# Layer 0 of a four-layer graph network: the order of key and value projections, bias halves and loads in its opening

## The chip, the cores and the metric

The kernel runs on one core of a Trainium2 chip. The metric is the device time of one execution in microseconds (us). The core has five engines that run side by side, each in its own order: PE (TensorE) multiplies matrices, DVE (VectorE) and ACT (ScalarE) do elementwise work and empty PE's accumulators, POOL (GpSimd) does some elementwise work and issues DMAs, SP (SyncE) only issues DMAs. Matrix products land in PSUM, a small accumulator memory; everything else on the chip lies in SBUF.

## What is computed

Four layers are applied in turn to a node matrix x of 4096 x 256 with a dense stored adjacency matrix adj of 4096 x 4096 (under 1% of its entries are not zero). Each layer's result is added to its input and normalized by row. Only the first layer is touched by the change:

```python
qkv = x @ Wqkv + bqkv                         # q, k, v: 4096 x 256 each, 4 heads of 64
scores = einsum('hnd,hmd->hnm', qh, kh) * 64 ** -0.5
scores = scores + graph_bias * adj
scores = where(adj == 0, -1e9, scores)
out = einsum('hnm,hmd->hnd', softmax(scores), vh)
x = layernorm(x + out @ Wout + bout)
```

(In the source the mask and the adjacency are two arguments; both are adj.) The second layer is a graph attention with one score per node and neighbour, the third and fourth multiply by the adjacency with normalized rows and columns.

## The kernel before, in words

**Tiles of layer 0.** The nodes are cut into 32 chunks of 128 query rows (class `Rows`, one per chunk). Two heads make a pair, so a chunk has two pairs (class `Pair`), and there are 64 units of work. The 4096 key columns are cut into four stretches of 1024, `k` = 0 to 3. One step is one unit and one stretch: 256 steps, and a few more to let the pipeline run out.

**What a step does.** `step(t)` writes out the order of the work by hand; the whole runs under `tc.manual_schedule()`, so each engine executes its instructions in the order in which the program issues them, and waits where one is not ready. Step t computes the scores of its own unit and stretch (`score`, L366: eight matmul records into two PSUM tiles), which DVE adds to the bias, writes to SBUF and takes the maximum of (L375, two instructions for two heads). Four steps behind, ACT takes exponentials (`expo`, L391); five steps behind, PE transposes them and ACT copies them out of PSUM (`turn`, L405 and L413); six steps behind, PE multiplies them by the values (`attend`, L423). So the first exponentials come in step 4, the first transposes in step 5, and the first attention in step 6.

**Bias rows.** Scores need, for each chunk, the bias `graph_bias * adj` with the mask. `Rows.load(k)` (L256) loads one stretch of the adjacency's rows in four DMAs on SP of 128 KB each, into one of two `raw` buffers. `make_bias(k, half)` handles half a stretch: DVE transposes it (L272), finds the zeros (L277) and forms the bias (L278). `make_edges` then lets ACT make a copy in bf16 for layer 1 and a row sum (L289) into one of two `mk` buffers, and POOL writes that to memory (L295). Bias tiles come from a pool of seven buffers, one of which holds the key and value weights `wkv_sb` as long as they are needed. From step 0 on, each step also makes half a stretch of the next chunk's bias.

**Queries.** `Rows.fetch` (L302, L306) loads the chunk's columns of the transposed x, `xq`, and its rows `xr`. `Rows.begin` projects the queries (L313, eight matmul records) into PSUM buffer `po1`, DVE moves them out with bias and scale (L321), and POOL adds the output bias to `xr` (L329).

**Keys and values.** They are projected from x in eight pieces of 512 nodes. `load_x(mb)` (L199) loads a piece of 512 KB on SP into one of five buffers. `project(mb)` computes two halves of the keys (L210, eight matmul records, PSUM buffers `po0` and `po1`), which ACT copies with the bias into `store` (L217; the first half serves pair 0), and then the values (L226, sixteen records, PSUM buffer `tr`), which DVE moves out with their bias (L233). The transposed exponentials use the buffer `tr` too.

**The opening before step 0.** SP gets, in this order: piece 0 of x, the weights `wkv_sb`, the first raw set of chunk 0, piece 1, the second raw set, `xq` and `xr`, pieces 2 and 3. Small constants, the query weights and the output weights go through ACT's queue. Then come the queries of chunk 0, and all eight bias halves of chunk 0, with `project(0)` and `project(1)` behind the second and the fourth half. In steps 1 to 3, ahead of the scores:

```python
if t > 0:
    for mb in range(2 * t, min(2 * t + 2, N // 512)):
        project(mb)
```

So step t's scores find all keys of their stretch, and pieces 2 to 7 stand in steps 1 to 3. `project(mb)` ends with the load of piece mb + 4.

Of the kernel before, what the change touches and what calls it, by code (L numbers as in the profile page):

```python
# [17 lines left out]
N = 4096  # L18
# [8 lines left out]
NS = N // TS  # L27
# [17 lines left out]
def tile_gnn(  # L45
# [123 lines left out]
    with ExitStack() as l0:  # L169
# [25 lines left out]
        x_in = {}  # L195

        def load_x(mb):
            xt = pp_.tile([P, 2, 512], F32, tag="pt", name="xt")
            nc.sync.dma_start(  # L199
                xt, xT[:, mb * 512 : (mb + 1) * 512].rearrange("(c p) m -> p c m", p=P)  # L200
            )
            x_in[mb] = xt

        def project(mb):

            xt = x_in.pop(mb)
            for pr in range(2):
                pk = ps_o.tile([P, 512], F32, tag=f"po{pr}", name="pk")
                for cc in range(2):
                    nc.tensor.matmul(  # L210
                        pk,
                        wkv_sb[:, cc, pr * P : (pr + 1) * P],
                        xt[:, cc, :],
                        start=(cc == 0),
                        stop=(cc == 1),
                    )
                nc.scalar.activation(  # L217
                    kT[:, pr, mb * 512 : (mb + 1) * 512],
                    pk,
                    AF.Identity,  # L220
                    bias=bqk_sb[:, 2 + pr : 3 + pr],
                )
            pv = ps_t.tile([P, 4, D], F32, tag="tr", name="pv")
            for s in range(4):
                for cc in range(2):
                    nc.tensor.matmul(  # L226
                        pv[:, s, :],
                        xt[:, cc, s * P : (s + 1) * P],
                        wkv_sb[:, cc, D : 2 * D],
                        start=(cc == 0),  # L230
                        stop=(cc == 1),
                    )
            nc.vector.tensor_tensor(  # L233
                v_sb[:, mb * 4 : (mb + 1) * 4, :],
                pv,
                bv_b.unsqueeze(1).to_broadcast([P, 4, D]),
                ALU.add,
            )
            if mb + 4 < N // 512:
                load_x(mb + 4)  # L240

        class Rows:

# [212 lines left out]
        rows = [Rows(ib) for ib in range(NCH)]  # L456
# [5 lines left out]
        def step(t):  # L462
            unit, k = divmod(t, NS)
            ib, pr = divmod(unit, 2)
            live = t < n_steps
            ua, ka = divmod(t - LA, NS)
            tag_a, tag_o = f"po{ua % 2}", f"po{1 - ua % 2}"
            ut, kt = divmod(t - LT, NS)
            ue, ke = divmod(t - LE, NS)
            attends = 0 <= ua < n_units  # L470
            turns = 0 <= ut < n_units
            expos = 0 <= ue < n_units
            grow = live and ib + 1 < NCH
            if grow and pr == 0 and k == NS - 1:
                rows[ib + 1].fetch()
            if ua > 0 and ka == 0:
                pairs[ua - 1].scale()
            if t > 0:
                for mb in range(2 * t, min(2 * t + 2, N // 512)):
                    project(mb)  # L480
            if live:
                if k == 0:
                    pairs[unit] = Pair(rows[ib], pr)
                pairs[unit].score(k)
            if expos:
                pairs[ue].expo(ke, 0)
            if turns:
                pairs[ut].turn(kt, 0)
            if expos:
                pairs[ue].expo(ke, 1)  # L490
            if attends:
                pairs[ua].attend(ka, tag_a)
                if ka == NS - 2:
                    pairs[ua].sums()
                if ka == NS - 1:
                    pairs[ua].norm(tag_o)
            if ua > 0 and ka == 1:
                if ua % 2 == 0:
                    pairs[ua - 1].rows.finish(tag_o)
                del pairs[ua - 1]  # L500
            if grow:
                if pr == 1 and k == NS - 2:
                    rows[ib + 1].begin(tag_o if attends else "po1")
                kb, half = divmod(pr * NS + k, 2)
                if edges:
                    edges.pop().make_edges()
                edges.append(rows[ib + 1])
                rows[ib + 1].make_bias(kb, half)
                if half == 0 and kb + 1 < NS:
                    rows[ib + 1].load(kb + 1)  # L510
                elif half == 0 and ib + 2 < NCH:
                    rows[ib + 2].load(0)
            elif edges:
                edges.pop().make_edges()
            if turns:
                pairs[ut].turn(kt, 1, by_dve=not live)
            for f, *args in tail.get(t, ()):
                f(*args)
# [98 lines left out]
        def first_es():  # L617
# [30 lines left out]
                (first_es,),  # L648
            ],
        }  # L650
        with tc.manual_schedule():
            load_x(0)
            nc.sync.dma_start(wkv_sb, wqkv[:, D:].rearrange("(c p) e -> p c e", p=P))
            rows[0].load(0)
            load_x(1)
            rows[0].load(1)
            rows[0].fetch()
            load_x(2)
            load_x(3)
            nc.scalar.dma_start(wout_sb, wout.rearrange("(c p) e -> p c e", p=P))  # L660
            nc.scalar.dma_start(bout_b, bout.partition_broadcast(P))
            rows[0].begin("po1")
            for k in range(NS):
                for half in range(2):
                    rows[0].make_bias(k, half)
                    rows[0].make_edges()
                if k < 2:
                    project(k)
                if k + 2 < NS:
                    rows[0].load(k + 2)  # L670
                elif k + 2 == NS:
                    rows[1].load(0)
            for t in range(n_steps + LA + 2):
                step(t)

# [444 lines left out]
```

## Time and profile before

| What | Value |
| --- | --- |
| Runs | 2788.17 us median of 3 (2787.74 to 2789.93) |
| Profiled execution | 2790.52 us, of which the span from first to last instruction is 2788.7 us |
| Busy share of the span | PE 98%, DVE 80%, ACT 59%, POOL 8% |
| First PE instruction | at 20.20 us |
| Start of the scores of steps 0, 1, 2, 3 | 36.69, 54.76, 70.65, 86.54 us |
| Start of the scores of step 7 | 107.38 us |

Times in the profile count from the first instruction. "x8" is a count of instructions, "L210" a line of the kernel, and `pk<-xt,wkv_sb` names what is written and read. Each matrix product in float32 appears as two matmul records. Matmuls overlap in PE's pipeline and their ends are modelled, so the busy time of a group can reach past the start of the next. The time in brackets is how long the engine was idle before the group, with what ended that idleness. The granted clock is the share of TensorE's full clock.

### The profile page before, as it was taken

What the parts mean: (1) busy time and instruction counts of PE and PEld (TensorE: products, weight loads), DVE (VectorE), ACT (ScalarE), POOL (GpSimd) and SP (SyncE); (2) the same over time, 40 slices, a digit from 0 to 9 for tenths busy, and PEclk for the clock granted to TensorE, in tenths of its full rate; (3) what the DMA queues carried; (4) which work ended last, traced back from release to release, by engine and by line L of the source; (5) the groups of instructions that cost most, each with busy time, mean ns of one, the idle gap of its engine ahead of it and who ended that gap; (6) DMA issues with size and microseconds to landing.
All of it is one profiled execution on the core that took longest, in us unless ns stands there. A gap on an engine that the chain in (4) does not pass through costs nothing.

```text
span 2788.7 us, 57962 instructions
## 1 busy us (share of the span) xinstructions
PE 2720.9 (98%) x23568; PEld 1862.4 (67%) x23568; DVE 2225.5 (80%) x4059; ACT 1655.4 (59%) x2675; POOL 234.3 (8%) x404
## 2 busy tenths in 40 slices
PE   6999999999999999999997999999999999999997
PEld 4677777777777777777786888886444444444443
DVE  4799999999988999999858888885866577676565
ACT  2699999999999999999857777772100001000000
POOL 1111111111111111111100000000200000000000
PEclk9999999999999999999999999999999999999998
DMA  6344444444444444444362222212555555555552
GB/s 156 63 83 86 93 87 85 89 90 83 87 92 83 88 89 84 90 87 87 95 202 70 77 77 76 76 43 90 176 158 170 162 159 157 164 168 175 181 169 73
DMA packets 671291, 308.01 MB, mean 110 GB/s; under 512 B 547376, under 2 KB 577456, under 8 KB 671024
## 3 DMA queue, kind: packets, MB, share of 16 engines
q1 hardware_dynamic: 655776, 265.10, 38.7%
q0 software_dynamic: 13440, 37.77, 3.5%
q8 instruction: 184, 3.01, 0.5%
q10 hardware_dynamic: 1808, 1.44, 0.2%
q14 instruction: 83, 0.68, 0.1%
HBM read 258.21 MB, written 46.01 MB: 109 GB/s over the span
## 4 chain that ended last, share of the span: by engine, by line
PE 93%; issue 3%; DVE 1%; DMA 1%; ACT 1%; SPq 0%; POOL 0%; DVEq 0%; POOLq 0%; ACTq 0%
PE m L948 27%; PE po L423 17%; PE po L770 16%; PE sc L366 16%; PE ptr L405 10%; PE py L982 2%; PE pq L313 1%; PE pp L335 1%; PE pb L441 1%; PE pk L210 1%; PE pv L226 1%; DMA mk<-edge 1%; SPq L256 0%; DMA x<-xs 0%; DVE z L375 0%
## 5 line engine op out<-in xcount | busy, mean ns | idle before, releaser
L375 DVE CUSTOM_DVE_ANT_0 z<-sc,bias 128x1024 f32<-128x1024 f32 x512 | 605.9, 1221 | 40.5 <-PE sc L366 39.0
L391 ACT ACTIVATE z<-z,nm 128x1024 f32<-128x1024 f32 x512 | 590.2, 1153 | 6.7 <-DVE nm L387 6.7
L413 ACT COPY pt<-ptr 128x1024 f32<-128x1024 f32 x507 | 511.4, 1009 | 99.3 <-PE ptr L405 89.9
L366 PE MATMUL sc<-store,qT 64*128 64x512 f32 x2048 | 506.7, 608 | 1.6 <-DVE mx L375 1.5
L423 PE MATMUL po<-pt,xc 128*64 128x128 f32 x8192 | 504.2, 276 | 0.0
L770 PE MATMUL po<-store,pt 128*128 128x257 f32 x2048 | 447.2, 380 | 12.6 <-issue 12.6
L423 PEld LDWEIGHTS po<-pt,xc 128*64 128x64 f32 x8192 | 442.3, 137 | 17.6 <-DVE pt L411 0.2
L405 PEld LDWEIGHTS ptr<-ident,z 64*128 64x128 f32 x8192 | 322.3, 138 | 177.8 <-issue 78.4
L770 PEld LDWEIGHTS po<-store,pt 128*128 128x128 f32 x2048 | 388.6, 190 | 70.9 <-issue 12.7
L948 PE MATMUL m<-asum,ysum 128*128 128x512 f32 x768 | 356.6, 594 | 6.3 <-issue 6.3
L405 PE MATMUL ptr<-ident,z 64*128 64x64 f32 x8192 | 356.3, 225 | 5.8 <-ACT pt L413 4.4
L366 PEld LDWEIGHTS sc<-store,qT 64*128 64x128 f32 x2048 | 192.9, 189 | 119.4 <-issue 109.2
L948 PEld LDWEIGHTS m<-asum,ysum 128*128 128x128 f32 x768 | 146.0, 190 | 177.9 <-issue 160.9
L948 PE MATMUL m<-asum,store 128*128 128x512 f32 x512 | 263.2, 596 | 0.0
L948 PE MATMUL m<-a,ysum 128*128 128x512 f32 x512 | 245.9, 594 | 0.0
L295 POOL DMA_DIRECT2D edge<-mk x256 | 145.4, 568 | 1004.5 <-ACT mk L289 981.1
L954 ACT COPY e<-m 128x512 f32<-128x512 f32 x32 | 18.5, 586 | 351.6 <-PE m L948 351.6
L917 DVE TENSOR_TENSOR asum<-a 128x512 f32<-128x512 f32 x128 | 88.1, 688 | 163.9 <-PE m L948 163.9
L724 ACT ACTIVATE z<-z,es_q 128x1024 f32<-128x1024 f32 x128 | 146.5, 1145 | 120.5 <-DVE mx L711 111.9
L278 DVE SCALAR_TENSOR_TENSOR bias<-rt,gb,u 128x512 f32<-128x512 f32 x256 | 194.2, 759 | 9.1
L760 DVE STREAM_TRANSPOSE pt<-z 128x1024 f32<-128x1024 f32 x128 | 158.1, 1237 | 41.7 <-PE po L770 41.7
L948 PEld LDWEIGHTS m<-asum,store 128*128 128x128 f32 x512 | 97.8, 191 | 123.3 <-issue 121.4
(123 smaller groups left out, 2561.5 us busy)
## 6 DMA issues: line engine op xcount, KB each, us to landing
a<-in_adjT SPq DMA_DIRECT2D x256, 512.0 KB, 5.1
raw<-in_adjT SPq DMA_DIRECT2D x512, 128.0 KB, 4.0
edge<-mk POOLq DMA_DIRECT2D x256, 128.0 KB, 2.5
mk<-edge SPq DMA_DIRECT2D x256, 128.0 KB, 2.9
xt<-in_xT SPq DMA_DIRECT2D x8, 512.0 KB, 5.4
xq<-in_xT SPq DMA_DIRECT2D x32, 128.0 KB, 3.9
xr<-in_x SPq DMA_DIRECT2D x32, 128.0 KB, 3.1
x<-xs POOLq DMA_DIRECT2D x8, 512.0 KB, 4.1
```

The source lines that it names most:

```text
L278: nc.vector.scalar_tensor_tensor(self.bias[k][:, m0 : m0 + HT], rt, gb, u, ALU.mult, ALU.add)
L295: nc.gpsimd.dma_start(edge[self.ib * P : (self.ib + 1) * P, k * TS + m0 : k * TS + m0 + HT], mk)
L366: nc.tensor.matmul(ps[j][:, q * 512 : (q + 1) * 512], self.rows.qT[j * HD : (j + 1) * HD, self.pr, :], kT[j * HD : (j + 1) * HD, self.pr, ...
L375: nc.vector.tensor_tensor_reduce(z, ps[j], self.rows.bias[k], 1.0, NEG, ALU.add, ALU.max, self.mx[:, j, k : k + 1],)
L391: nc.scalar.activation(z, z, AF.Exp, bias=self.nm[:, j : j + 1], accum_out=self.ls[:, j, k : k + 1],)
L405: nc.tensor.transpose(pa[:, r, c, :], z[half, c * P : (c + 1) * P], ident[half, half])
L413: nc.scalar.copy(to, pa)
L423: nc.tensor.matmul(self.po[j * HD : (j + 1) * HD, 0:P], v_sb[:, ci, h * HD : (h + 1) * HD], self.pt[j][k][:, c, :], start=(ci == 0), stop= ...
L724: nc.scalar.activation(self.z[s], self.z[s], AF.Prelu, bias=self.eq[:, s : s + 1], alpha=SLOPE)
L760: nc.vector.transpose(self.pt[:, :, s, :], self.z[s].rearrange("p (b r) -> p b r", r=QB))
L770: nc.tensor.matmul(self.po[:, 0 : D + 1], self.pt[:, b, :, :].rearrange("p s i -> p (s i)"), wh[:, b, :], start=(b == 0), stop=(b == NBK - 1),
L948: nc.tensor.matmul(self.m[i], left, right, start=(c == 0), stop=(c == NP - 1))
```

## The change

`project` is split into `project_k` (keys) and `project_v` (values). Before step 0, SP's queue gets `xq` and `xr` before piece 1, and five pieces of x instead of four; `project_v(mb)` then loads piece mb + 5. Before step 0 the kernel projects the keys of pieces 0 and 1, with the queries of chunk 0 between them, and makes two bias halves instead of eight. The other six, all values and the keys of pieces 2 to 7 are put into a plan for steps 0 to 4, which `step` executes directly behind the step's scores. The first raw set of chunk 1 is asked for before step 0 as before, but ahead of the third and fourth of chunk 0, which follow in steps 0 and 1; chunk 1's second set follows at the end of step 1 and its third at the end of step 2.

```diff
-        def project(mb):
-
-            xt = x_in.pop(mb)
+        def project_k(mb):
+
+            xt = x_in[mb]
             for pr in range(2):
                 pk = ps_o.tile([P, 512], F32, tag=f"po{pr}", name="pk")
...
                     AF.Identity,
                     bias=bqk_sb[:, 2 + pr : 3 + pr],
                 )
+
+        def project_v(mb):
+
+            xt = x_in.pop(mb)
             pv = ps_t.tile([P, 4, D], F32, tag="tr", name="pv")
...
-            if mb + 4 < N // 512:
-                load_x(mb + 4)
+            if mb + 5 < N // 512:
+                load_x(mb + 5)
...
-            if t > 0:
-                for mb in range(2 * t, min(2 * t + 2, N // 512)):
-                    project(mb)
             if live:
                 if k == 0:
                     pairs[unit] = Pair(rows[ib], pr)
                 pairs[unit].score(k)
+            for f, *args in plan.get(t, ()):
+                f(*args)
             if expos:
                 pairs[ue].expo(ke, 0)
...
                 rows[ib + 1].make_bias(kb, half)
-                if half == 0 and kb + 1 < NS:
+                if t < NS:
+
+                    if t == 1:
+                        rows[0].load(3)
+                    if 0 < t < 3:
+                        rows[1].load(t)
+                elif half == 0 and kb + 1 < NS:
                     rows[ib + 1].load(kb + 1)
...
+        def first_bias(k, half):
+            rows[0].make_bias(k, half)
+            rows[0].make_edges()
+            if k == 1 and half == 1:
+                rows[0].load(2)
+
+
+        plan = {}
+        for t in range(3):
+            plan[t] = [
+                (project_v, 2 * t),
+                (project_k, 2 * t + 2),
+                (first_bias, t + 1, 0),
+                (project_v, 2 * t + 1),
+                (project_k, 2 * t + 3),
+                (first_bias, t + 1, 1),
+            ]
+        plan[3] = [(project_v, 6)]
+        plan[4] = [(project_v, 7)]
         with tc.manual_schedule():
             load_x(0)
             nc.sync.dma_start(wkv_sb, wqkv[:, D:].rearrange("(c p) e -> p c e", p=P))
             rows[0].load(0)
+            rows[0].fetch()
             load_x(1)
             rows[0].load(1)
-            rows[0].fetch()
-            load_x(2)
-            load_x(3)
+            for mb in range(2, 5):
+                load_x(mb)
...
+            project_k(0)
             rows[0].begin("po1")
-            for k in range(NS):
-                for half in range(2):
-                    rows[0].make_bias(k, half)
-                    rows[0].make_edges()
-                if k < 2:
-                    project(k)
-                if k + 2 < NS:
-                    rows[0].load(k + 2)
-                elif k + 2 == NS:
-                    rows[1].load(0)
+            project_k(1)
+            for half in range(2):
+                rows[0].make_bias(0, half)
+                rows[0].make_edges()
+            rows[1].load(0)
             for t in range(n_steps + LA + 2):
                 step(t)
```

## The prediction

> **What bounds the kernel now.** I read the page's share by engine first (PE 98% of 2788.7 us), then the busy time by stage, then each engine's instructions in order of time for the first 130 us, then SP's queue. By stage (columns: stretch and its length, busy us of PE, PE's weight loads, DVE, ACT and POOL, granted clock, DMA share, GB/s):
> ```profile
> 20.00:24.00 4.00, 3.80 (x11) 2.73 (x12) 1.65 (x4) 0.43 (x1) 0.73 (x1) 1.00 0.94 356
> 36.69:54.76 18.07, 16.15 (x57) 9.63 (x57) 13.64 (x21) 6.03 (x14) 3.60 (x7) 1.00 0.77 168
> 54.76:70.65 15.89, 15.89 (x58) 9.73 (x57) 6.62 (x9) 3.36 (x6) 0.54 (x1) 1.00 0.31 66
> 70.65:86.54 15.89, 15.89 (x58) 9.73 (x57) 6.63 (x9) 3.36 (x6) 0.54 (x1) 1.00 0.03 10
> 86.54:107.38 20.84, 18.00 (x139) 10.01 (x138) 16.65 (x29) 11.58 (x21) 1.98 (x4) 0.84 0.37 64
> 107.38:1340.00 1232.62, 1232.62 (x17560) 931.04 (x17556) 1126.05 (x2193) 1153.22 (x1898) 185.54 (x325) 1.00 0.43 87
> ```
> From 107.38 us to 1340 PE is never idle. The change touches only what lies before, so whatever it takes from 107.38 should come off the end unshortened. The earlier stretches are steps 0 to 2 and then steps 3 to 6, each measured from the start of its scores. PE in order of time (start, us, operation, count, [idle before it and its releaser]):
> ```profile
> 20.20 2.07 PE L313 MATMUL pq<-xq,w_sb 128*128 128x128 f32 x8 [20.20 <-DMA xq<-in_xT]
> 22.07 4.35 PE L210 MATMUL pk<-xt,wkv_sb 128*128 128x512 f32 x8
> 26.25 3.62 PE L226 MATMUL pv<-wkv_sb,xt 128*128 128x256 f32 x16
> ...
> 36.69 1.99 PE L366 MATMUL sc<-store,qT 64*128 64x512 f32 x8
> ...
> 47.68 3.70 PE L210 MATMUL pk<-xt,wkv_sb 128*128 128x512 f32 x8 [1.92 <-ACT store L217]
> ...
> 86.54 1.99 PE L366 MATMUL sc<-store,qT 64*128 64x512 f32 x8
> 89.84 4.12 PE L366 MATMUL sc<-store,qT 64*128 64x512 f32 x8 [1.32 <-DVE mx L375]
> ```
> PE does nothing for 20.20 us: its first operation is the query projection, and xq comes late. Then it projects and scores without a break but for 1.92 us, and from 86.54 it has little to do and waits for DVE. SP's queue says why xq is late (start, us, operation, count):
> ```profile
> 5.61 5.39 SPq L256 DMA_DIRECT2D raw<-in_adjT  x4
> 11.04 0.89 SPq L199 DMA_DIRECT2D xt<-in_xT  x1
> 11.97 4.21 SPq L256 DMA_DIRECT2D raw<-in_adjT  x4
> 16.22 0.87 SPq L302 DMA_DIRECT2D xq<-in_xT  x1
> 17.14 0.47 SPq L306 DMA_DIRECT2D xr<-in_x  x1
> 17.65 1.46 SPq L199 DMA_DIRECT2D xt<-in_xT  x3
> ```
> xq is issued at 16.22, behind eight loads of 128 KB in 128-byte packets. The first xt (issued 0.75, 5.7 us to landing) and wkv_sb (1.24, 6.6 us) are there at 6.5 and 7.9 us, unused.
>
> **What the skill says.** The Trainium skill, "DMA: Bandwidth & Descriptors", "Issuing engines are not separate DMA queues": all queues share 16 DMA engines. Its "Why small descriptors are slow" adds a fixed overhead per packet. The trace agrees: 157 GB/s between 10 and 14 us, nearly all 128-byte packets, against 356 between 20 and 24, nearly all 2 KB, with the engines full both times. So the order of SP's queue decides when xq and xt land. "TensorE: Matmul & The Clock Gate", Part 1: an idle PE starts at half clock and needs about 3.4 us of activity. The trace agrees: the first eight query matmuls took 2.07 us and later ones 1.16, and the clock is 0.84 in the starved stretch from 86.54. The same page, "Architectural detail", calls ACT and DVE strict first-in-first-out; the 1.92 us is such a case (below).
>
> **The change, part by part.** k, v stand for one key or value projection (8 matmul records, 3.43 to 3.70 us; 16, 3.45 to 3.62), sc for a step's scores (1.92), T0, T3, T7 for the start of the scores of steps 0, 3, 7: now 36.69, 86.54, 107.38.
>
> 1. *SP's queue at the start.* xq (0.87 us of issue) and xr (0.47) move ahead of xt(1) and the second raw set; a fifth xt follows the fourth. The first raw set is untouched. xq is then issued at 11.04 where xt(1) was. Its 256 packets and xr's 128 took about 1.5 us of the DMA engines, so xq lands at 11.04 + 3.9 = 14.9, and xt(1), which landed at 11.04 + 4.9 = 15.9, at about 17.4. xt(2) to (4) land as before, by 25, since the bytes ahead of them are the same; they are wanted after 27.
> 2. *PE's start.* k(0) starts at 7.9 instead of 20.20. Cold, its 3.43 us take up to 6.9, so it ends by 14.8. The queries start at 14.9 and take 1.1 to 2.1; k(1) waits for xt(1) at 17.4 and ends at 20.9 warm, or 22.6 with one cold window of 3.4 us (half of it lost). I take T0 = 21.5. DVE doesn't hold it: queries off PSUM by 17.6, then two half biases of 1.87 by 21.4, wanted at T0 + 2 by the first score eviction. Gain to T0: 36.69 - 21.5 = 15.2, but two v (6.9) have only been put behind it.
> 3. *Steps 0 to 2.* Each still holds sc, two k, two v: 15.89 of PE, as in the rows from 54.76 and 70.65. Step 0 took 18.07, with the 1.92 wait: the key copies (L217) stood behind an ACT mask copy (L289) that waited 3.1 us for an edge DMA, as six bias halves ran back to back into two mk buffers. In the new plan a k and a v lie between halves (6.9 us against 2.2 to 4.6 us of an edge's landing), so the wait goes; nothing is late in its place. T0 to T3: 49.85 now, 3 x 15.89 = 47.67 after; gain 2.2. DVE gets per step two score evictions (2.29), two v evictions (2.3), three bias halves (5.6): 10.2 of 15.89, so all of the six moved bias halves are hidden under projections. If that cover were gone they would cost 11.2. What moves with them: on ACT three mask copies a step (0.82 each with the read of the sum) beside four key copies (0.69), 5.2 of 15.89; on POOL three edge issues (0.56) and their landings, spread wider than now.
> 4. *Steps 3 to 6.* v(6), v(7), 6.9 us of PE and 2.3 of DVE, come here. PE from T3 = 0: sc to 1.9, v(6) to 5.4, sc to 7.3, v(7) to 10.8, sc to 12.7. DVE: evictions to 4.3, maximum 4.5, v(6) to 6.7, bias to 8.6, evictions to 10.9, v(7) to 12.1, bias to 14.0, evictions to 16.3, bias to 18.2, evictions of step 6 to 20.5. PE's attention and queries of step 6 end at about 21.5, and so T7 is at T3 + 21.8, against 20.84 now: the values fill PE time that DVE leaves open. Cost 1.0; from 0 (DVE's chain hides all; the clock of 0.84 goes up with a busier PE, so a small gain isn't excluded) to 6.9 (nothing hidden). One buffer comes into it: wkv_sb holds one of the seven bias buffers until v(7) has run, and the bias of step 4 takes that buffer; since DVE evicts v(7) before it writes that bias anyway, this adds no wait.
> 5. *Rows' loads on SP.* raw(0,2) is issued when bias (1,1) has been transposed, at T0 + 14.4. Four loads need 6.1 us from first issue to last landing (25.44 to 31.55 now): T0 + 20.5, wanted at T0 + 22.6, behind v(2)'s eviction. raw(0,3) goes out at T0 + 32.2, lands at T0 + 38.3, is wanted at T0 + 38.5. Ahead of them on SP stand loads of xt(5), (6) that wait for v(0), v(1), done earlier. A late raw set holds DVE's bias half and, behind it, a v eviction and the next score evictions; PE notices after DVE's slack of 5.7 us. I count 0; rows[1]'s loads are a step later than now with 6 us in hand.
> 6. *A new wait.* sc of steps 0 to 3 now follows directly on a k whose ACT copy it reads (before, a v lay between). The half that pair 0 reads is copied (0.69) while PE does the other half (1.7), so I count 0. If the scores must wait for both copies, 0.9 us each, 3.6 in all. A wait can't be below 0.
>
> Sum: 15.2 + 2.2 - 1.0 = 16.4. T7 goes from 107.38 to about 91.0. The profiled span of 2788.7 (execution 2790.52, so 1.8 lie around it) becomes 2772.3; the median of the runs, 2788.17, is 0.5 under that span, and gives 2771.8. I say 2772.
>
> **Rivals.** What a measurement can tell from no change is about 0.2%, 5.6 us.
> - *The new wait of part 6.* PE idles 0.9 us four times on L217: gain 12.8, 2775.4. For it: the scores read what ACT has just written. Against: the copy of the needed half has 1.7 us of cover.
> - *Little hidden in steps 3 to 6, or a cold start.* DVE becomes the bound with v's evictions, or PE, starved of xt between 13 and 17 us, starts its long run at half clock: 3 to 6 us lost, about 2777. For it: DVE was 80% busy in steps 3 to 6. Against: its sum above, 20.5 us, barely reaches PE's.
> - *The late rows: slower.* SP serves in order, and raw(0,2) and (0,3) are issued only a few us before use. To end over 2793.7, the two must cost PE 22 us, so 11 each, beyond DVE's 5.7 us: each set would have to land some 17 us after it is wanted. The longest landing of a raw load in the opening was 6.7 us. For it: no slack in my reckoning for raw(0,3). Against: a microsecond or two late only shifts DVE inside its slack.
> - *The change doesn't do what it says:* k(0) is held by something that the trace doesn't show, and PE starts at 15 rather than 8. Then k(0) ends by 18.5, k(1) by 24 to 25, gain about 13: still faster.
>
> **How the numbers follow.** Forecast (2769.5 to 2774.5) 0.57; the new wait 0.13; little hidden, cold or late start 0.18; more gain than reckoned (k(1) warm and early, steps 3 to 6 no longer than now: to 2768 and below) 0.04; late rows or another order of waits that eats it to within 0.2%: 0.03; slower 0.05. The range from 2768 to 2779 holds the first three but for tails. Faster 0.92, same 0.03, slower 0.05.
>
> **What would show it.** Right: PE's first operation is L210 at about 8; the queries wait for xq until about 15; scores first at 21 to 22.5; no idle before L210 in step 0; steps 0 to 2 of 15.9; L226 between the fourth and sixth scores; T7 near 91, and 1233 us of PE without idle from there. Wrong: idle on PE before L366 with releaser ACT store L217 (part 6), DVE waiting for DMA raw (part 5), T3 to T7 over 24 (part 4), clock under 1 past 17 us (part 2).

## The result, and the profile after

The changed kernel takes 2774.95 us (median of 4 runs, 2772.64 to 2776.13) against 2788.43 (4 runs, 2787.74 to 2789.93): a ratio of 0.9950, 95% interval 0.9933 to 0.9967. A later series on another occasion gave 2771.79 (5 runs) against 2788.35 (8 runs): 0.9940, 0.9926 to 0.9954. The forecast was 2772 with a range of 2768 to 2779, which holds both; its narrower range, 2769.5 to 2774.5, holds the second and misses the first by 0.45. The profiled span fell from 2788.7 to 2772.5 us.

PE in order of time, of the changed kernel (start, us, operation, count, [idle before it and its releaser]; L370 are the scores now, L230 the values, L317 the queries):
```profile
7.93 5.06 PE L210 MATMUL pk<-xt,wkv_sb 128*128 128x512 f32 x8 [7.93 <-DMA wkv_sb<-in_wqkv]
14.55 1.13 PE L317 MATMUL pq<-xq,w_sb 128*128 128x128 f32 x8 [1.56 <-DMA xq<-in_xT]
17.52 5.40 PE L210 MATMUL pk<-xt,wkv_sb 128*128 128x512 f32 x8 [1.84 <-DMA xt<-in_xT]
22.85 1.99 PE L370 MATMUL sc<-store,qT 64*128 64x512 f32 x8
24.77 3.72 PE L230 MATMUL pv<-wkv_sb,xt 128*128 128x256 f32 x16
28.32 3.60 PE L210 MATMUL pk<-xt,wkv_sb 128*128 128x512 f32 x8
...
70.51 1.99 PE L370 MATMUL sc<-store,qT 64*128 64x512 f32 x8
72.43 3.72 PE L230 MATMUL pv<-wkv_sb,xt 128*128 128x256 f32 x16
76.08 1.99 PE L370 MATMUL sc<-store,qT 64*128 64x512 f32 x8
```
SP's queue of the changed kernel (start, us, operation, count):
```profile
5.09 5.69 SPq L260 DMA_DIRECT2D raw<-in_adjT  x4
10.83 0.86 SPq L306 DMA_DIRECT2D xq<-in_xT  x1
11.73 0.47 SPq L310 DMA_DIRECT2D xr<-in_x  x1
12.24 0.43 SPq L199 DMA_DIRECT2D xt<-in_xT  x1
```
PE starts with keys at 7.93, when the weights land; xq is issued at 10.83 instead of 16.22. Of the first 20.20 us that it stood idle before, 7.93 are left, and two gaps of 1.56 and 1.84 us, each ended by the DMA that the prediction named. The busy times by stage (stretch and its length, busy us of PE, PE's weight loads, DVE, ACT and POOL, granted clock, DMA share, GB/s):
```profile
22.85:38.73 15.88, 15.88 (x57) 9.72 (x56) 8.65 (x13) 4.58 (x10) 2.67 (x5) 1.00 0.64 164
38.73:54.62 15.89, 15.89 (x57) 9.73 (x56) 10.22 (x16) 3.97 (x8) 1.08 (x2) 1.00 0.37 86
54.62:70.51 15.89, 15.89 (x57) 9.72 (x56) 10.22 (x16) 4.58 (x10) 2.53 (x5) 1.00 0.53 91
70.51:93.12 22.61, 21.39 (x169) 14.23 (x170) 19.85 (x33) 14.21 (x28) 3.81 (x7) 1.00 0.56 109
93.12:1330.00 1236.88, 1236.88 (x17618) 933.99 (x17616) 1130.41 (x2202) 1157.17 (x1906) 185.70 (x326) 1.00 0.43 87
```
The first three rows are steps 0 to 2: the 18.07 us of step 0 are gone. The fourth is steps 3 to 6, with the two value projections in it: 1.77 us longer than before, and PE's busy time in it is 21.39 where it was 18.00. From T7 at 93.12, where it was 107.38, PE is never idle up to the end of the stretch. So 14.26 us were gained in the opening.

The span fell by 16.2, 1.9 more. The trace shows where 1.6 of it is: from T7 to the start of the last scores of layer 0 the kernel before took 1290.4 us and this one 1288.8. 30 us near the end of layer 0, begun at the same point of the work (14.26 us earlier), before and then after:
```profile
1370.00:1400.00 30.00, 28.00 (x386) 19.85 (x382) 20.19 (x49) 26.11 (x36) 2.70 (x5) 0.94 0.33 104
```
```profile
1355.74:1385.74 30.00, 28.00 (x414) 20.62 (x412) 21.76 (x51) 27.51 (x38) 2.69 (x5) 1.00 0.33 108
```
Before, a window at half clock fell into it (0.94 on the mean of 30 us), after, none did, and PE got through 414 matmul records instead of 386. Of the eleven runs below, three took 1290.3 to 1290.4 us for the stretch and eight 1288.8. The three have T7 at 89.3, 101.0 and 102.6 us, the eight have it anywhere from 86.2 to 104.6. So the change doesn't need to be its cause, though so few single traces can't rule out a link, and this part of the span isn't counted as the change's gain.

### The profile page after: what moved, and what is told of

Its sections match the earlier page's. It is cut to its first block, busy times and chain, and to the rows that moved or that the text cites. A ratio compares the mean times of both kernels' runs of the same rounds, so it can differ in the third digit from the quotient of the medians.

```text
span 2772.5 us, 57962 instructions
## 1 busy us (share of the span) xinstructions
PE 2717.1 (98%) x23568; PEld 1859.7 (67%) x23568; DVE 2226.1 (80%) x4059; ACT 1654.8 (60%) x2675; POOL 233.9 (8%) x404
## 4 chain that ended last, share of the span: by engine, by line
PE 93%; issue 3%; DVE 1%; DMA 1%; ACT 0%; SPq 0%; POOL 0%; DVEq 0%; POOLq 0%; ACTq 0%
PE m L973 27%; PE po L427 17%; PE po L795 16%; PE sc L370 16%; PE ptr L409 10%; PE py L1007 2%; PE pq L317 1%; PE pp L339 1%; PE pv L230 1%; PE pk L210 1%; PE pb L445 1%; DMA xt<-in_xT 0%; DMA mk<-edge 0%; DMA x<-xs 0%; POOL x L577 0%
## 5 line engine op out<-in xcount | busy, mean ns | idle before, releaser
L370 PE MATMUL sc<-store,qT 64*128 64x512 f32 x2048 | 502.0, 604 | 0.1
L370 PEld LDWEIGHTS sc<-store,qT 64*128 64x128 f32 x2048 | 191.4, 188 | 117.2 <-issue 110.9
```

What stands on the lines that cost most here:

```text
L370: nc.tensor.matmul(ps[j][:, q * 512 : (q + 1) * 512], self.rows.qT[j * HD : (j + 1) * HD, self.pr, :], kT[j * HD : (j + 1) * HD, self.pr, ...
```

## The experiments

T0, T3 and T7 are the starts of the scores of these steps, read from each run's own trace. "Keys 0" and "keys 1" are the times that the keys of pieces 0 and 1 took; the last column is the profiled execution. All in us:

| Kernel | Keys 0 | Keys 1 | T0 | T3 | T7 | Execution |
| --- | --- | --- | --- | --- | --- | --- |
| Before | 4.35 | 3.60 | 36.69 | 86.54 | 107.38 | 2790.52 |
| Changed | 5.06 | 5.40 | 22.85 | 70.51 | 93.12 | 2774.30 |
| The queue alone | 4.55 | 3.60 | 31.83 | 81.71 | 102.60 | 2782.60 |
| The queue undone | 5.38 | 4.66 | 27.18 | 74.84 | 97.46 | 2777.70 |
| Values in step 2 | 5.17 | 5.28 | 22.89 | 79.05 | 101.03 | 2781.11 |
| All bias halves ahead | 5.42 | 5.40 | 23.18 | 81.95 | 104.56 | 2784.89 |
| PE kept busy | 6.14 | 3.60 | 20.93 | 68.59 | 91.21 | 2772.72 |
| Late rows | 5.21 | 5.40 | 23.18 | 70.85 | 93.46 | 2774.54 |
| x ahead of the rows | 5.99 | 3.60 | 19.07 | 66.73 | 89.34 | 2769.30 |
| A bias half earlier | 6.12 | 3.70 | 21.79 | 69.45 | 92.07 | 2772.87 |
| Values 7 behind the half | 6.71 | 3.70 | 20.66 | 68.32 | 90.07 | 2770.69 |
| The best version | 3.67 | 3.70 | 16.80 | 64.47 | 86.22 | 2767.66 |
| Changed, second execution | 5.94 | 3.70 | 20.96 | 68.62 | 91.24 | 2772.51 |

The two executions of the changed kernel differ by 1.9 us at T0 and T7, of which 1.7 are the keys of piece 1. A difference of T0 or T7 below 2 us between two runs shows nothing by itself; differences inside a stretch such as T3 to T7 are steadier (22.61 and 22.62 in these two).

**The queue alone.** In the kernel before:
```diff
             rows[0].load(0)
+            rows[0].fetch()
             load_x(1)
             rows[0].load(1)
-            rows[0].fetch()
```


> One part alone: the kernel before with only xq and xr moved ahead of piece 1 of x on SP's queue; keys, values and bias halves stand as before. By the sum of the prediction, xq lands at 14.4 as in the changed kernel, PE starts there with the queries, and two projections of keys and values follow: scores of step 0 at about 31 instead of 36.69. The wait of step 0 stays, at 2 to 3 us, since the eight bias halves still stand ahead of the key copies. T7 at about 102, so 5 to 5.5 of the 14.3 us that the change took from 107.38. If the queue alone were the cause and the reordering of keys and values worth nothing, T7 would be near 93; if the queue were worth nothing, near 107.


PE (lines left out are marked):
```profile
15.17 2.05 PE L313 MATMUL pq<-xq,w_sb 128*128 128x128 f32 x8 [15.17 <-DMA xq<-in_xT]
...
31.83 1.99 PE L366 MATMUL sc<-store,qT 64*128 64x512 f32 x8
...
42.85 3.70 PE L210 MATMUL pk<-xt,wkv_sb 128*128 128x512 f32 x8 [1.94 <-ACT store L217]
```
T0 31.83, T7 102.60. The queue is worth 4.8 of the 14.3 us, and the wait of step 0 stays, 1.94 instead of 1.92: the two are separate parts.

**The queue undone.** The same lines turned round in the changed kernel: `rows[0].fetch()` back behind `rows[0].load(1)`.


> One part undone: the changed kernel with xq and xr back behind the second raw set. By the sum, keys of piece 0 still start at 7.9, then PE idles for about 7 us, the queries start cold at 20.2 and take 2.1, keys of piece 1 end at about 26.3: T0 26.3 instead of 22.85, T7 96.6 instead of 93.12. If the place of xq didn't matter because piece 1 of x comes late anyway, T7 would stay near 93.


T0 27.18, T7 97.46. PE stands still for 7.75 us between the keys of piece 0 and the queries, which start at 20.75 and take 2.04:
```profile
20.75 2.04 PE L317 MATMUL pq<-xq,w_sb 128*128 128x128 f32 x8 [7.75 <-issue]
```
The queue is worth 4.3 us here against the first execution of the changed kernel and 6.2 against the second. With 4.8 in the old order these agree within the 2 us by which executions of one kernel differ, so the two parts roughly add up. The rest of the change without the queue took T7 from 107.38 to 97.46, 9.9 us: it is the larger part.

**The values of pieces 6 and 7 in step 2.** In the changed kernel:
```diff
-        plan[3] = [(project_v, 6)]
-        plan[4] = [(project_v, 7)]
+        plan[2] += [(project_v, 6), (project_v, 7)]
```


> One part undone: the changed kernel with the values of pieces 6 and 7 at the end of step 2 instead of in steps 3 and 4. If they hide in time that DVE's chain leaves open, as the prediction says, T3 comes 6.9 us later (77.4) and the stretch T3 to T7 goes back to about 20 to 21 us from 22.61: T7 about 97.5 to 98.5, 4.5 to 5.5 us later than in the changed kernel. If little is hidden (the rival), T3 to T7 shrinks to about 16 and T7 stays near 93.


PE:
```profile
75.40 3.72 PE L230 MATMUL pv<-wkv_sb,xt 128*128 128x256 f32 x16 [1.32 <-DVE xc L237]
79.05 1.99 PE L370 MATMUL sc<-store,qT 64*128 64x512 f32 x8
83.45 3.13 PE L370 MATMUL sc<-store,qT 64*128 64x512 f32 x8 [2.41 <-DVE mx L379]
87.80 3.88 PE L370 MATMUL sc<-store,qT 64*128 64x512 f32 x7 [1.23 <-DVE mx L379]
```
T3 79.05, T7 101.03: 7.9 us later than the changed kernel, where I had expected 4.5 to 5.5. T3 to T7 is 21.98 without the values, 22.61 with them: 7 us of PE cost 0.6 us against this run and 1.77 against the kernel before (20.84). The 21.98 isn't free of the values, though: DVE still evicts those of piece 7 and makes a bias half behind T3, and reaches the first scores 3.1 us after T3, where it takes 2.0 in the changed kernel. So they hide well, and how well lies between the two figures. In step 2 they cost more than their own time: the two value projections stand directly behind each other, and the second waits until DVE has emptied the one PSUM buffer (1.32 us). The rival with little hidden falls.

**All bias halves ahead of step 0.** In the changed kernel:
```diff
-                (first_bias, t + 1, 0),
...
-                (first_bias, t + 1, 1),
...
-            for half in range(2):
-                rows[0].make_bias(0, half)
-                rows[0].make_edges()
-            rows[1].load(0)
+            for k in range(NS):
+                for half in range(2):
+                    rows[0].make_bias(k, half)
+                    rows[0].make_edges()
+                if k + 2 < NS:
+                    rows[0].load(k + 2)
+                elif k + 2 == NS:
+                    rows[1].load(0)
```
(and the rows' loads inside the steps in their old order).


> One part undone: the changed kernel with all eight bias halves of chunk 0 ahead of step 0, with the rows' loads in their old order. By the prediction the spreading hides six halves under projections. Without it DVE reaches the first score eviction only when the eighth half is done, at about 36 to 38 instead of 24.87, the first values stay in PSUM until about 40, and PE waits for that buffer: step 0 some 8 to 9 us longer, T7 about 101 to 102. If the spreading only removes the 1.92 us wait, T7 is about 95.


PE's step 0, and its stage:
```profile
40.64 6.17 PE L230 MATMUL pv<-wkv_sb,xt 128*128 128x256 f32 x16 [8.38 <-DVE xc L237]
```
```profile
23.18:50.17 26.99, 18.61 (x57) 11.40 (x56) 15.81 (x24) 7.92 (x20) 5.39 (x10) 0.81 0.68 155
```
T7 104.56, 11.4 us later. The mechanism is the expected one: DVE reached the first score eviction at 37.08 and the first value eviction at 39.36, and the second values waited 8.38 us for the buffer. Of DVE's delay 5.4 us are waits of its own, 3.9 for raw sets and 1.5 for ACT's mask copies. What I had not counted is the clock: it was at half from 35.40 to 45.64 us (0.81 on the mean of the step), and the values took 6.17 instead of 3.6 us. That the 11.4 us come close to the 11.2 which the prediction named for a lost cover is chance: 8.4 of them are the wait and 2.6 the clock. So the spreading isn't just the removal of a 1.92 us wait. Without it only 2.8 of the 14.3 us are left; with the keys first it is what makes the early start usable.

**PE kept busy in its gaps.** In the changed kernel, `fill(n)`: n matmuls of the 128 x 128 identity with itself into the values' PSUM buffer, which nobody reads:
```diff
             project_k(0)
+            fill(6)
             rows[0].begin("po1")
+            fill(7)
             project_k(1)
```


> The disputed cost by itself: the changed kernel with 6 and 7 matmuls of the identity with itself, read by nobody, in PE's two idle stretches (1.56 us before the queries and 1.84 us before the keys of piece 1). If the half clock from 17.6 to 21.0, which made those keys 5.40 us instead of 3.43, comes from PE's idleness before it, they take 3.4 to 3.6 now: T0 21.0 instead of 22.85, T7 91.2. If the window falls there whatever PE does, T0 stays at 22.9.


The keys of piece 1 start at 17.40 and take 3.60 us; T0 20.93, T7 91.21, as computed. For the keys of piece 1, the changed kernel's stage, then this run's:
```profile
17.52:22.85 5.33, 5.33 (x9) 2.08 (x9) 2.47 (x4) 0.69 (x1) 0.00 (x0) 0.68 0.90 234
```
```profile
17.40:20.93 3.53, 3.53 (x11) 1.34 (x9) 2.87 (x5) 0.69 (x1) 0.00 (x0) 1.00 1.02 226
```
A clock of 0.68 against 1.00, the DMA as busy in both. This doesn't show that the filling did it. The second execution of the changed kernel, with nothing filled in, had no half clock there either:
```profile
17.33 3.70 PE L210 MATMUL pk<-xt,wkv_sb 128*128 128x512 f32 x8 [1.37 <-DMA xt<-in_xT]
```
Seven executions have this opening unfilled. In four (the changed kernel, values in step 2, all bias halves ahead, late rows) the clock fell behind the queries and the keys of piece 1 took 5.28 to 5.40 us; in three they took 3.70. In the four, the half clock began behind 3.4 us in which PE was busy for only 1.13 to 1.26 (in the changed kernel it lasts from 17.55 to 20.97, behind 14.14 to 17.55). In the four the keys of piece 0 had taken 5.06 to 5.42 us, in the three 5.94 to 6.71, and in the filled run 6.14: it may have been spared without filling. So the half clock costs the keys of piece 1 1.7 us where it comes; which execution it comes in, and whether filling prevents it, stays open.

**Late rows.** In the changed kernel, the fourth raw set loaded twice over and behind the other chunk's:
```diff
-                    if t == 1:
-                        rows[0].load(3)
                     if 0 < t < 3:
                         rows[1].load(t)
+                    if t == 1:
+                        rows[0].load(3, 2)
```


> The suspected wait made longer: the changed kernel with the fourth raw set of chunk 0 loaded twice over and behind chunk 1's second set on SP's queue, so that it lands some 6 to 7 us later (about 65 to 66 instead of 58.9; wanted by DVE at 61.4). By the prediction DVE's slack in step 2 takes this in: DVE waits 4 to 5 us, PE not at all, T3 stays at 70.5 and T7 within 0.7 us of 93.12. By the rival of the late rows PE would stall in step 2 or 3 and T7 come 4 us or more later.


Who waited for whom on DVE, from 20 us to T7 (us in total, times, longest):
```profile
DVE xc L237 <- PE pv L230: 12.2, 7, 3.8
DVE z L379 <- PE sc L370: 5.9, 3, 5.1
DVE rt L276 <- DMA raw<-in_adjT: 4.8, 1, 4.8
```
DVE waited 4.8 us for the set and began on it at 66.63, where the changed kernel's DVE never waits for rows. T0 to T3 is 47.67 (47.66 in the changed kernel) and T0 to T7 70.28 (70.27): PE saw nothing of it. The mechanism of the slower rival needs far more lateness than this change brings.

**x ahead of the rows.** In the changed kernel (`fetch_rows` is the load of xr, split off):
```diff
-            rows[0].load(0)
             rows[0].fetch()
             load_x(1)
-            rows[0].load(1)
-            for mb in range(2, 5):
-                load_x(mb)
+            rows[0].load(0)
+            load_x(2)
+            rows[0].fetch_rows()
+            rows[0].load(1)
+            load_x(3)
+            load_x(4)
```


> One order changed: the changed kernel with xq, then piece 1 of x, ahead of the first raw set on SP's queue, piece 2 behind it, and xr and the second raw set after that. If T0 is set by the landing of xq and piece 1 alone, PE runs keys, queries, keys without a break from 7.9: T0 at 17.6 to 18, T3 47.7 later, T7 at 88 to 88.5, so 4.7 to 5.2 us off the changed kernel. DVE's first bias then starts about 2 us later and the first score eviction at 20 to 21; that is in time for PE's next use. If DVE's bias rather than xq and piece 1 sets the pace, T1 - T0 grows beyond 15.9 by what T0 gained.


PE:
```profile
7.78 5.99 PE L210 MATMUL pk<-xt,wkv_sb 128*128 128x512 f32 x8 [7.78 <-DMA wkv_sb<-in_wqkv]
14.54 1.16 PE L322 MATMUL pq<-xq,w_sb 128*128 128x128 f32 x8 [0.78 <-ACT store L217]
15.54 3.60 PE L210 MATMUL pk<-xt,wkv_sb 128*128 128x512 f32 x8
19.07 1.99 PE L375 MATMUL sc<-store,qT 64*128 64x512 f32 x8
```
T0 19.07, T7 89.34: 3.8 us off the changed kernel instead of the 4.7 to 5.2 expected, and 1.9 off its second execution, which had no half clock in the keys of piece 1 either. Both waits, for xq and for piece 1, are gone, and T1 - T0 is 15.88, so DVE holds nothing up. (Lines stand five further down here: L322 are the queries, L375 the scores.) In their place come a longer cold start (5.99 us) and 0.78 us in which the queries wait until ACT has emptied their PSUM buffer of keys. So the order of the loads still held T0 back in the changed kernel, by about 2 us when the clock is alike.

**A bias half earlier; then the values of piece 7 behind the bias half.** In the changed kernel, first chunk 1's half of step 3 made in step 2:
```diff
+                if t in (2, 3):
+                    kb, half = 1, 1
+                if t != 3:
                     edges.append(rows[ib + 1])
                     rows[ib + 1].make_bias(kb, half)
...
+        def next_bias():
+            edges.pop().make_edges()
+            rows[1].make_bias(1, 0)
+            rows[1].make_edges()
+
+        plan[2].insert(3, (next_bias,))
```
and in a second kernel also the values of piece 7 at the end of step 4 (`tail` is what `step` does last):
```diff
-        plan[4] = [(project_v, 7)]
+        tail[4] = [(project_v, 7)]
```


> One size changed: the changed kernel with the bias half of chunk 1 that DVE makes in step 3 moved into step 2 (one half of 1.87 us more there, where DVE is idle for 3.8 us in the middle). If DVE's chain bounds steps 3 to 6, the stretch T3 to T7 of 22.61 shrinks by 1 to 1.9: T7 91.2 to 92.1. If PE's own work bounds it, T7 stays at 93.1.

> The bias half of chunk 1 moved from step 3 to step 2 as in the run before, and the values of piece 7 put behind step 4's bias half, so that DVE does that half while PE still computes those values. If the stretch T3 to T7 is bound by a chain that starts anew at the end of these values (their eviction, then the bias half, then the score evictions of step 5), the eviction of step 5's first score starts about 1 us earlier and PE loses its 0.85 us wait inside the scores of step 6: T3 to T7 21.7 to 21.9 instead of 22.61. If something else bounds it, it stays at 22.6.


The first left T3 to T7 at 22.62: a miss. DVE had 1.9 us less to do there and nothing became shorter. The chain that ended last, of that first run, shows why (start, us, what):
```profile
77.01 3.67 PE pv L230 x16
80.67 0.02 issue
80.69 0.06 DVE xc L237
...
81.83 0.71 DVE rt L276
82.55 0.02 issue
82.57 0.44 DVE u L281
83.01 0.02 issue
83.03 0.75 DVE bias L282
83.79 1.14 DVE z L379
84.92 0.02 DVE mx L379
```
The chain runs over DVE only from the end of the values of piece 7 on: their eviction, the bias half behind it, the score eviction, and then PE's next scores. What DVE does earlier only makes it wait longer for those values. In the second run DVE does the bias half while PE still computes the values; step 5's first eviction starts 13.2 us after T3 instead of 14.3, and T3 to T7 is 21.75, as expected. That eviction in the changed kernel (T3 70.51), then in this run (T3 68.32):
```profile
84.77 1.22 DVE L379 CUSTOM_DVE_ANT_0 z<-sc,bias 128x1024 f32<-128x1024 f32 x1
```
```profile
81.48 1.23 DVE L379 CUSTOM_DVE_ANT_0 z<-sc,bias 128x1024 f32<-128x1024 f32 x1 [0.19 <-PE sc L370]
```

**The best version.** The order of the loads of the run above, both edits of the last one, the queries in the other PSUM buffer, and
```diff
+            fill(14)
             project_k(0)
-            rows[0].begin("po1")
+            rows[0].begin("po0")
```


> A version meant to beat both kernels: xq and piece 1 of x ahead of the first raw set, as tried; 14 matmuls of the identity with itself, read by nobody, from about 1.5 to 7.5 us, so that PE's clock is up when the weights land; the queries in the other PSUM buffer; and the two edits of the run with the values of piece 7 behind the bias half. Keys of piece 0 at 7.8 to 11.3, queries to 12.4, keys of piece 1 from their landing at 13.3: T0 16.8, T3 64.5, T7 86.3. Against the kernel before 21 us at T7, so about 2767 on the scale of 2788; the changed kernel 14.3 us. If the clock stays at half until it has seen real work, T0 is about 19 and T7 88.5.

> The changed kernel itself, for the best version to be compared with on the same chip, and for a narrower interval: 0.9950, 13 to 16 us under the kernel before; T0 22 to 23, T7 92 to 93.5.


PE of the best version:
```profile
1.37 4.82 PE L683 MATMUL fill<-ident 128*128 128x128 f32 x28 [1.37 <-POOL ident masks.py:199]
7.91 3.67 PE L210 MATMUL pk<-xt,wkv_sb 128*128 128x512 f32 x8 [1.72 <-DMA wkv_sb<-in_wqkv]
11.42 1.05 PE L322 MATMUL pq<-xq,w_sb 128*128 128x128 f32 x8
13.17 3.70 PE L210 MATMUL pk<-xt,wkv_sb 128*128 128x512 f32 x8 [0.70 <-DVE qT L330]
16.80 1.99 PE L375 MATMUL sc<-store,qT 64*128 64x512 f32 x8
```
T0 16.80, T3 64.47, T7 86.22, each within 0.1 us of what was computed. For T0 that is partly luck: the keys of piece 1 were to wait for their load until 13.3, and waited until 13.17 for DVE to move the queries out of the PSUM buffer that they now share with the keys. It takes 2767.36 us (5 runs, 2766.45 to 2769.13), 0.9924 of the kernel before, interval 0.9911 to 0.9937; the changed kernel beside it took 2771.79, T0 20.96, T7 91.24. So 5.0 us more at T7 (4.2 of them up to T0, 0.9 in steps 3 to 6), and 4.4 in the medians; the slowest of its runs is faster than the fastest of the changed kernel's (2771.26). What each of its edits adds is not shown apart.

## Why the prediction was right

The sum was 15.2 + 2.2 - 1.0 = 16.4 us at T7; measured in the two profiles of the changed kernel were 14.3 and 16.1, and 13.5 and 16.6 in the medians of the two series. The parts were right in kind: the queue, the keys first, the bias halves spread, the values in steps 3 to 6. That the first profile's span (2772.5) comes within 0.2 us of the forecast one (2772.3) is luck: T7 was 2.1 us late, and 1.9 us came off behind T7, which the prediction had at nothing.

1. *The queue.* xq was to land at 14.9 and piece 1 at 17.4; PE's two waits on them ended at 14.55 and 17.52. The experiments put the queue at 4.3 to 6.2 us.
2. *PE's start.* T0 was forecast as 21.5 between 20.9 and 22.6; it was 22.85 and, in the later run, 20.96. The term between them is the clock, which the prediction had as "one cold window"; it came in one of the two executions.
3. *Steps 0 to 2.* 47.67 forecast, 47.66 measured, and no idle before L210. That the 1.92 us wait goes because the bias halves are spread is argued, not shown alone. In the run that keeps them together PE waits 8.4 us, for the values' buffer. There, too, ACT copies keys late, at 41.98 us, behind mask copies and 9.7 us after PE was done with these keys, but the longer wait covers it.
4. *Steps 3 to 6.* This is the term that was mis-sized: 21.8 forecast, 22.61 measured. I had the right chain, values of piece 7, their eviction, a bias half, score evictions, but with 3.45 us for a value projection where each step of scores and values takes 5.57, which puts the end of the values at T3 + 11.2 instead of 10.8; that is half of the 0.8. The other half lies behind the evictions of step 5. PE's weight loads wait 0.85 us between these, inside the scores of step 6:
```profile
87.19 0.30 PEld L370 LDWEIGHTS sc<-store,qT 64*128 64x128 f32 x4 [0.85 <-DVE mx L379]
```
From here to T7 it took 5.9 us, where I had 5.5. My sentence that "the values fill PE time that DVE leaves open" was right, as the run with the values in step 2 shows, and the clock of this stretch rose from 0.84 to 1.00.
5. *Rows' loads.* Counted at 0; DVE never waited for a raw set, and 4.8 us of made waiting cost PE nothing.
6. *The new wait.* No idle of PE before L370 in steps 0 to 3. Ahead of step 0 ACT copies the needed half from 21.24 to 21.93, while PE does the other half; the other copy starts at 22.95, when the scores have begun at 22.85.

The rivals: the new wait didn't come; the cold start came, in one of two profiles of the changed kernel, at 1.7 us; little hidden and late rows were refuted by their own runs; the keys of piece 0 were held by nothing unseen, PE started at 7.93. The Trainium skill's half clock ("TensorE: Matmul & The Clock Gate", Part 1) carried the argument in part 2, and the first keys bear it out (5.06 and 5.94 us instead of 3.43). The second start doesn't fit the page's terms. It puts the half clock behind an idle window of about 3.4 us; here the clock fell behind gaps of 1.56 and 1.84 us with 1.1 us of work between them, and did not in another execution with gaps of 1.09 and 1.37. The measurement decides: shorter gaps can be enough.

## What to carry to other kernels

When one engine is busy without a break from some point on, price a change before that point by when that point comes. What differs behind it, here 1.9 us, is then not yet the change's. In an opening, order each queue by what the bound engine can start with, and give slow loads that are only needed a stage later the later places. Work on a second engine that looks like the bound shortens nothing if the bound engine's own result restarts its chain: look for the last such restart, and move what stands behind it.

## What the runs showed of the hardware that was not expected

While PE stood idle for 8.4 us the granted clock fell to half, at 35.40 us, and stayed there until 45.64: the value projection behind the pause took 6.17 instead of 3.6 us, so the pause cost 2.6 us more than its length. The first key projection took 5.06 to 6.71 us in the ten runs that start with it, the same work each time; in the one run that puts 28 matmul records on an identity ahead of it (1.37 to 6.2 us) it took 3.67. The views don't show this first cold stretch as a low clock: in the changed kernel they give 1.00 from 7.00 to 12.99 us, where these keys took 5.06, so a cold start is read from durations. A half-clock window at the end of layer 0 came in four of thirteen traces and cost 1.6 us each time, with the same program work there.
